# One maximum for both parts of a shared score bank, masks for it by TensorE, and rows of the next batch listed a step ahead of their transposes

## The chip, the cores and the metric

The kernel runs on one core of a Trainium2 chip. The time is the device time of one execution in microseconds (us); less is better. The core's engines work from queues of their own: TensorE (PE in the profile; its weight loads are PEld), VectorE (DVE), ScalarE (ACT), GpSimd (POOL), and SyncE (SP), which issues DMAs here. TensorE writes into PSUM, which has eight banks of 128 partitions by 512 float32 values; an engine waits where it needs data or a buffer that another still holds.

## The reference

A transformer block with adaptive layer norms: attention, then a mixture of experts, over 4 batches of 1024 tokens of width 256.

```python
h = _layernorm(x) * (1 + ca) + sa
x = x + ga * attention(h)          # 16 heads of width 16, causal
h = _layernorm(x) * (1 + cb) + sb
x = x + gb * experts(h)            # 8 experts, the two best of each token

# attention
scores = jnp.einsum('bhqd,bhkd->bhqk', Q, K) / np.sqrt(D_HEAD)
causal = jnp.triu(jnp.full((t, t), -jnp.inf), k=1)
attn = jax.nn.softmax(scores + causal, axis=-1)
O = jnp.einsum('bhqk,bhkd->bhqd', attn, V)
```

The softmax subtracts each query's largest score. The kernel needs that maximum before it computes the scores that it exponentiates, and this is the work that the change touches.

## The kernel before

The attention runs over 16 units: unit u is batch u // 4 and, within it, four heads (`qd` = u % 4). Scores are computed twice. The first time (`m_parts`, L822) queries lie on the partitions, and VectorE takes each query's maximum over the keys (`maxima`, L837). `max_rows` (L857) turns the maxima into rows with a transpose on TensorE and writes them by DMA into a spare row of the query tile. The second time (`s_parts`, L889) keys lie on the partitions, the spare row subtracts the maximum inside the matmul, ScalarE takes the exponential (`weigh`, `exponential`), and `av_step` (L924) multiplies by the values.

A unit has nine steps. In step i, `both` (L1087) does the exponentiated scores of unit u and the maxima of unit u + 1, in two halves of two heads each. A half-step on TensorE is: two score banks and two maxima banks filled in turn, the masks on the scores (L913), then the value product of the step before (first half), or a piece of other work (second half). Each head has a contraction of 32 rows, so four matmuls run side by side in the array. A matmul in float32 is two records in the profile.

All these banks, and those of smaller work (`misc`), come from one pool of seven PSUM buffers, `ps_sc`. A bank is free again when ACT has taken its exponential or DVE its maximum.

`m_steps` (L801) says which query tile (128 queries) and key half (512 keys) each step's maxima bank holds, as (query tile, key half, first column). Causality leaves some tiles narrow, and in steps 1, 2 and 8 two of them share a bank: 384 + 128, 256 + 256, and 384 + 128 columns. The last 128 columns of a tile on the diagonal need the triangular mask. In `both` VectorE adds the mask in the same custom operation that takes the maximum (L851), one per part and head, each followed by a read of its accumulator; tiles off the diagonal take a plain reduction (L849, tile `mf`), and the second key half's maximum includes the first's through `mf`. Before unit 1's third step, `m_alone` (L870) does maxima with TensorE adding the masks (L878). There, and on the scores, a mask is a bf16 matmul of an identity and the mask (`unit`, `qmask`).

The other work is kept in queues, and a few pieces are taken after each step. `todo` has the next batch's layer norm and projections: `ln_pieces` (L719) gives the statistics and four pieces, one per half of the tokens and half of the width, that transpose normalized rows; then come query and key projections (`qk_pieces`) and value projections (`v_pieces`). The rows `xn` of one half (`normalized`, L62, four operations of VectorE) are made in the first piece of that half, in a tile with one buffer (`xnp`). `spread` (L786) sends projected queries and keys by DMA to the tiles of a unit, two units ahead. The number of pieces after a step is what is left divided by the steps left, rounded up; in the last batch it is two. `gates`, `choices` and `sends` are further queues, with the gates of the attention and the routing.

The order in the text is not wholly the order on the engines: the compiler's scheduler may move an instruction ahead of others of its engine where its data allow it. Statistics and row operations can so come earlier than they are written.

After the attention (from about 760 us) comes the expert stage, which the change does not touch.

Of the kernel before, what the change touches and what calls it, by code (L numbers as in the profile page):

```python
# [9 lines left out]
F32 = mybir.dt.float32  # L10
# [51 lines left out]
def normalized(nc, pool, x_b, mv, rs, half, tag):  # L62

    xn = pool.tile([P, 4, D], F32, tag=f"xn{tag}", name=f"xn{tag}")
    for i in range(4):
        t = 4 * half + i
        nc.vector.tensor_scalar(
            xn[:, i, :], x_b[:, t, :], mv[:, t, 0:1], rs[:, t : t + 1], ALU.subtract, ALU.mult
        )
    return xn  # L70
# [10 lines left out]
def adaln_block_kernel(  # L81
# [495 lines left out]
    with ExitStack() as actx:  # L577
# [130 lines left out]
        def blank_rows():  # L708
# [7 lines left out]
            for rows in (blank, slots[JUNK : JUNK + BLK, :]):  # L716
                nc.sync.dma_start(out=rows.rearrange("(p j) d -> p j d", p=P), in_=fill)

        def ln_pieces(b):  # L719
            def begin():  # L720
                st["ln", b], pieces = layer_norm_pieces(nc, small, xs[b], eps, "a")
                for f in pieces:
                    f()
                st["hT", b] = htp.tile([P, NDC, T], F32, tag="hT", name="hT")

            def piece(half, dc):
                def run():
                    if dc == 0:
                        st["xn", b] = normalized(nc, xnp, xs[b], *st["ln", b], half, "a")
                        if b == 0 and half == 0:  # L730
                            modulated(st.pop("ps_m"))
                    transposed(
                        nc, misc(), st["xn", b], dc, ident,
                        st["hT", b][:, dc, half * 512 : (half + 1) * 512],
                        scale1[:, dc, b : b + 1], modT[:, dc, b : b + 1],
                    )

                return run

            out = [piece(h, dc) for h in range(NH) for dc in range(NDC)]  # L740
            return [lambda f=out[0]: (begin(), f())] + out[1:]
# [44 lines left out]
        def spread(u):  # L786
# [16 lines left out]
            [(4, 0, 0)], [(6, 0, 0)], [(7, 0, 0)], [(7, 1, 0)], [(6, 1, 0), (4, 1, 384)],  # L803
        ]

        s_steps = [
            [(0, 0, 0)], [(0, 1, 0), (0, 3, 384)], [(0, 2, 0), (1, 6, 256)],
            *([(1, kt, 0)] for kt in range(5)), [(1, 5, 0), (1, 7, 384)],
# [3 lines left out]
        def in_turn(*heads):  # L812

            for k in range(max(map(len, heads))):
                for parts in heads:
                    for f in parts[k : k + 1]:
                        f()
# [4 lines left out]
        def m_parts(u, i, j, open_end=False):  # L822

            ps, r = bank("ps_max"), HW * j

            def fill(k):
                qt, kb, at = m_steps[i][k]
                n = m_size(qt, kb)
                nc.tensor.matmul(  # L829
                    ps[:, at : at + n], qTs[u % 3][r : r + HW, qt * P : (qt + 1) * P],  # L830
                    kTs[u % 3][r : r + HW, kb * 512 : kb * 512 + n],
                    start=(k == 0), stop=(k == len(m_steps[i]) - 1 and not open_end),
                )

            return ps, [lambda k=k: fill(k) for k in range(len(m_steps[i]))]

        def maxima(u, i, j, ps, masked=()):  # L837

            for part in sorted(m_steps[i], key=lambda part: (part in masked, part[2]), reverse=True):
                qt, kb, at = part
                half, n = qt // 4, m_size(qt, kb)
                kind = ("mx", u, half) if kb == half else ("mf", u)
                if kind not in st:
                    st[kind] = mxp.tile([P, 4, 4], F32, tag=kind[0], name=kind[0])
                top = st[kind][:, j, qt % 4 : qt % 4 + 1]
                if kb < half or part in masked:
                    nc.vector.tensor_reduce(top, ps[:, at : at + n], AX.X, ALU.max)  # L849
                else:  # L850
                    nc.vector.tensor_tensor_reduce(  # L851
                        out=unused[:, 0:n], in0=ps[:, at : at + n], in1=cmask[:, 512 - n : 512], scale=1.0,
                        scalar=st["mf", u][:, j, qt % 4 : qt % 4 + 1] if kb else MASKED,
                        op0=ALU.add, op1=ALU.max, accum_out=top,
                    )

        def max_rows(u, half):  # L857

# [207 lines left out]

        todo = deque()
        soon = deque()

        gates, choices, sends = deque(), deque(), deque()  # L1070
        pending = None
# [15 lines left out]
        def both(u, i, u_max, i_max):  # L1087

            pts = []
            for h in range(2):  # L1090
                scores, tops, parts = [], [], []
                for j in (2 * h, 2 * h + 1):
                    for of, banks in ((s_parts(u, i, j), scores), (m_parts(u_max, i_max, (j + 2) % 4), tops)):
                        banks.append(of[0])
                        parts.append(of[1])
                in_turn(*parts)
                for k in range(2):
                    maxima(u_max, i_max, (2 * h + k + 2) % 4, tops[k])
                pts.extend(weigh(i, scores, h == 0))

                if h == 0 and pending is not None:
                    finish(pending)
            return u, i, pts


# [32 lines left out]
        for u in range(NU):  # L1138
            b, qd = divmod(u, NQD)
            if u + 2 < NU:  # L1140
                spread(u + 2)()
            if u > 0 and qd == 0 and b + 1 < B:
                st["rest"] = ln_pieces(b + 1) + qk_pieces(b + 1, 0), v_pieces(b + 1) + qk_pieces(b + 1, 1)
            if b + 1 < B:
                one, two = st["rest"]
                if u > 0:
                    todo.extend((one[:10], one[10:], two[:10], two[10:])[qd])
            if qd == 1 and 0 < b < B - 1:
                todo.extend(wo_pieces(b - 1))
            if qd == 0:  # L1150
                biases, weights = gate_pieces(b)
                if u > 0:
                    gates.extend(biases)
            if qd == 2 and b < B - 1:
                gates.extend(weights)
            if u == NU - 2:
                for k in range(B):
                    nc.sync.dma_start(out=gb[:, k, :], in_=mods[k, 1, :].partition_broadcast(P))
            if qd == 2 and 0 < b < B - 1:
                choices, sends = map(deque, route_pieces(b - 1, misc))  # L1160
            for i in range(BEGUN if u == 0 else 0, len(s_steps)):
# [12 lines left out]
                if (b, qd, i) == (B - 1, 1, 4):  # L1174
                    gates.extend(weights)

                pending = both(u, i, u + 1, i) if u + 1 < NU else four_heads(u, i)
                if u + 1 < NU and i == 4:
                    todo.appendleft(max_rows(u + 1, 0))

                if gates:
                    gates.popleft()()
                while soon and soon[0][0] <= step:
                    soon.popleft()[1]()

                for _ in range(2 if b == B - 1 else -(-len(todo) // (len(s_steps) - i))):
                    if todo:
                        todo.popleft()()
                early = b == B - 1 and (qd, i) < (1, 2)
                sending = early or not choices  # L1190
                for _ in range(1 if early else 2 - i % 2 if b > 1 else 1 + (i % 3 == 2)):
                    if choices and not (early and len(choices) < 19):
                        choices.popleft()()
                for _ in range(2 if u + 1 == NU or u == NU - 4 and i % 2 else 1):
                    if sends and sending:
                        sends.popleft()()
                step += 1
            while b + 1 < B and len(todo) > 1:
                todo.popleft()()
            if u + 1 < NU:  # L1200
                todo.appendleft(max_rows(u + 1, 1))
# [161 lines left out]
```

## Time and profile before

| | us |
|---|---|
| median of 3 runs | 1061.35 (1058.91 to 1062.14) |
| the profiled execution | 1067.35 |
| its span, first to last instruction | 1065.6 |
| TensorE busy in the span | 1009.5 (95%) |
| VectorE busy | 750.8 (70%) |
| ScalarE busy | 509.7 (48%) |
| plain maxima, L849, of 512 columns, 256 of them | 164.0 |
| maxima with mask, L851, of four widths, 488 of them | 254.8 (140.5 and 114.3 in two groups) |
| masks on the scores, L913, 1328 of them | 57.5 |

The profile is one execution. Its page has the span in 40 equal slices (26.6 us each), a digit for each engine's busy share in tenths. Groups are instructions of one line, engine and shape: count, total busy time, mean of one in nanoseconds, idle time before them and what ended it. A timeline is in order of time: start, length, engine, line, what is written and read, count of merged instructions, and idle time before. Matmuls overlap in the array, so a record's length is more than its share of the engine's time; the distance from one start to the next is what a matmul costs when TensorE is full.

### The profile page before, as it was taken

How to read it: one execution, taken by the hardware profiler on the slowest of the kernel's cores; microseconds unless marked ns; L12 is line 12 of the kernel's file. 1: busy time of each engine (PE TensorE's matmuls, PEld its weight loads, DVE VectorE, ACT ScalarE, POOL GpSimd, SP SyncE). 2: the span in 40 equal slices, each digit the busy share in tenths (PEclk: the TensorE clock that was granted, in tenths of full speed). 3: DMA queues.
4: the chain of work that ended last, by engine and by line, in shares of the span. 5: the costliest groups of instructions: out<-in, count | busy, mean ns of one | idle time of the engine just before them, and what ended most of it. 6: DMA issues, size and time to landing. Idle time of an engine off the chain costs nothing. (4 is left out here: it accounts for less than half of the span.)

```text
span 1065.6 us, 22453 instructions
## 1 busy us (share of the span) xinstructions
PE 1009.5 (95%) x8154; PEld 597.5 (56%) x8154; DVE 750.8 (70%) x2349; ACT 509.7 (48%) x963; POOL 239.5 (22%) x231
## 2 busy tenths in 40 slices
PE   5899999999999999999999999998689999999994
PEld 4554534544544544454463444533368888888893
DVE  4787867766787877788868788782466686566761
ACT  4125654655555555655545546446313264444540
POOL 4000010000000001222001330015131764444344
PEclk9899999999999999999999999999889999999997
DMA  8310120110111202123010331002489956443432
GB/s 272 82 31 8 38 47 14 35 39 14 38 46 49 56 24 48 45 65 86 19 42 28 78 83 36 22 28 72 135 260 289 314 105 158 72 66 65 66 62 25
DMA packets 68686, 81.58 MB, mean 77 GB/s; under 512 B 19480, under 2 KB 50072, under 8 KB 68448
## 3 DMA queue, kind: packets, MB, share of 16 engines
q1 hardware_dynamic: 55008, 63.26, 21.7%
q0 software_dynamic: 13296, 16.89, 8.9%
q8 instruction: 64, 1.05, 0.4%
q14 instruction: 46, 0.38, 0.1%
q10 hardware_dynamic: 272, 0.00, 0.0%
HBM read 45.11 MB, written 24.93 MB: 66 GB/s over the span
## 5 line engine op out<-in xcount | busy, mean ns | idle before, releaser
L921 ACT ACTIVATE pt<-ps_s 128x512 f32<-128x512 f32 x576 | 313.0, 596 | 295.0 <-PE ps_s L913 183.2
L829 PE MATMUL ps_max<-kT,qT 32*128 32x512 f32 (+3 forms) x1536 | 376.6, 531 | 4.6 <-DVE mf L849 2.9
L896 PE MATMUL ps_s<-qT,kT 32*128 32x512 f32 (+3 forms) x1536 | 343.9, 527 | 4.2 <-DMA qT<-rows 2.4
L896 PEld LDWEIGHTS ps_s<-qT,kT 32*128 32x128 f32 x1536 | 134.5, 186 | 143.3 <-issue 44.9
L849 DVE TENSOR_REDUCE mf<-ps_max 128x1 f32<-128x512 f32 x256 | 164.0, 682 | 60.4 <-PE ps_max L829 55.2
L851 DVE CUSTOM_DVE_ANT_0 unused<-ps_max,cmask,mf 128x256 f32<-128x256 f32 (+3 forms) x256 | 140.5, 549 | 46.9 <-PE ps_max L829 27.1
L829 PEld LDWEIGHTS ps_max<-kT,qT 32*128 32x128 f32 x1536 | 153.4, 188 | 34.3 <-DVE mx L851 11.0
L940 PE MATMUL av<-pt,vaug 128*32 128x512 f32 (+3 forms) x1536 | 160.3, 505 | 0.8 <-ACT ot L948 0.8
L972 POOL TENSOR_TENSOR oc<-oc,rec 64x512 f32<-64x512 f32 x32 | 40.6, 1270 | 506.9 <-DMA rec<-inv 453.8
L567 POOL DMA_INDIRECT out_dram<-y,xb x67 | 107.8, 1609 | 131.1 <-DVE gs L529 55.7
L851 DVE CUSTOM_DVE_ANT_0 unused<-ps_max,cmask 128x128 f32<-128x128 f32 (+2 forms) x232 | 114.3, 493 | 29.5 <-PE ps_max L829 15.1
L550 PE MATMUL ps_h<-xt,wa 128*128 128x256 f32 (+1 forms) x608 | 125.2, 358 | 1.3 <-DVE xt L538 1.3
L561 PE MATMUL ps_y<-wb,hs 128*128 128x256 f32 x536 | 122.7, 379 | 0.0
L550 PEld LDWEIGHTS ps_h<-xt,wa 128*128 128x128 f32 x608 | 103.6, 193 | 12.3 <-DVE xt L538 1.6
L561 PEld LDWEIGHTS ps_y<-wb,hs 128*128 128x128 f32 x536 | 100.6, 190 | 13.2 <-ACT hs L554 0.2
L529 DVE SCALAR_TENSOR_TENSOR gs<-x,share,gs 128x256 f32<-128x256 f32 x201 | 85.2, 477 | 1.0
L554 ACT ACTIVATE hs<-ps_h 128x512 f32<-128x512 f32 x67 | 39.8, 597 | 86.4 <-PE ps_h L550 76.9
L940 PEld LDWEIGHTS av<-pt,vaug 128*32 128x32 f32 x1536 | 38.1, 112 | 76.4 <-issue 67.4
L343 POOL DMA_INDIRECT slots<-hr,sloti x64 | 63.7, 995 | 76.5 <-ACT sloti L342 55.5
L566 DVE TENSOR_TENSOR y<-ps_y,gs 128x256 f32<-128x256 f32 x67 | 25.9, 419 | 72.2 <-PE ps_y L561 69.6
L913 PEld LDWEIGHTS <-qmask 128*32 128x32 bf16 (+1 forms) x1328 | 30.2, 97 | 66.6 <-issue 59.1
L913 PE MATMUL ps_s<-unit,qmask 128*32 128x128 bf16 (+1 forms) x1328 | 57.5, 227 | 0.1
(220 smaller groups left out, 924.2 us busy)
## 6 DMA issues: line engine op xcount, KB each, us to landing
w_s<-in_w_dram SPq DMA_DIRECT2D x16, 512.0 KB
xb<-slots SPq DMA_DIRECT2D x29, 259.0 KB
qT<-qc SPq DMA_DIRECT2D x64, 64.0 KB
kT<-kc SPq DMA_DIRECT2D x64, 64.0 KB
oc<-ot SPq DMA_DIRECT2D x128, 32.0 KB
rec<-inv SPq DMA_DIRECT2D x32, 128.0 KB
out_dram<-x SPq DMA_DIRECT2D x8, 512.0 KB
wa<-in_w_dram SPq DMA_DIRECT2D x8, 512.0 KB
```

Source lines behind the costliest of these rows:

```text
L343: sent = nc.gpsimd.indirect_dma_start(out=slots, out_offset=bass.IndirectOffsetOnAxis(ap=at, axis=0), in_=hr[:, t, :], in_offset=None,).ins
L529: nc.vector.scalar_tensor_tensor(gs[:, j, :], gb[:, b, :], share[:, j, b : b + 1], gs[:, j, :], ALU.mult, ALU.add)
L550: nc.tensor.matmul(ps[:, k, :], w[:, dc, fc * P : (fc + 1) * P], xt[:, dc, :], start=(dc == 0), stop=(dc == NDC - 1),)
L561: nc.tensor.matmul(ps[:, j, :], hs[:, fc, j * P : (j + 1) * P], w[:, fc, :], start=(fc == 0), stop=(fc == NFC - 1),)
L567: added = nc.gpsimd.indirect_dma_start(out=out_rows, out_offset=bass.IndirectOffsetOnAxis(ap=xb[:, j, D : D + 1].bitcast(I32), axis=0), in ...
L829: nc.tensor.matmul(ps[:, at : at + n], qTs[u % 3][r : r + HW, qt * P : (qt + 1) * P], kTs[u % 3][r : r + HW, kb * 512 : kb * 512 + n], sta ...
L849: nc.vector.tensor_reduce(top, ps[:, at : at + n], AX.X, ALU.max)
L851: nc.vector.tensor_tensor_reduce(out=unused[:, 0:n], in0=ps[:, at : at + n], in1=cmask[:, 512 - n : 512], scale=1.0, scalar=st["mf", u][:, ...
L896: nc.tensor.matmul(ps[:, at : at + n], kTs[u % 3][r : r + HW, kt * P : (kt + 1) * P], qTs[u % 3][r : r + HW, (qb + 1) * 512 - n : (qb + 1) ...
L913: nc.tensor.matmul(ps[k : k + w, at : at + P], qmask[:, k : k + w], unit, start=False, stop=at == masked[-1],)
L921: nc.scalar.activation(pt[:, 0:n], ps[:, 0:n], AF.Exp)
L940: nc.tensor.matmul(av[HW * j : HW * (j + 1), 512 - n : 512], vaug[b % 2][:, kt, 4 * qd + j, :], pts[j][:, at : at + n], start=(kt == 0), s ...
```

## The change

It has three parts.

**Maxima of two parts at once.** For units above 4 (`joint`), the steps whose bank holds two parts let TensorE add the masks to the maxima banks, and VectorE takes one plain reduction over the whole bank into two or four maxima (`joint_maxima`), as a bank of 256 + 256 or as four pieces of 128. Partial maxima of the 384-column tile go to a tile `mp`; `join` reduces and combines them after steps 2 and 8. Both halves' maxima lie in one tile `mx2`. Steps 0 and 3 change places for these units, so that one half is whole after step 2.

**Statistics in units 1 and 2.** The layer norm statistics of batches 2 and 3 are listed one piece per step from unit 1 on.

**Rows a step ahead.** For batches 2 and 3 the first half's rows are listed at the end of the unit before, and the second half's right behind the last transposes of the first half, a step ahead of their own transposes. In the first four steps of the units at which a batch's projections begin (4 and 8), one piece is taken per step, two in the first.

```diff
+        m_joint = [m_steps[3], *m_steps[1:3], m_steps[0], *m_steps[4:]]
+        def joint(u):
+            return u > NQD
+        def m_list(u):
+            return m_joint if joint(u) else m_steps
...
+        def joint_maxima(u, i, j, ps):
+            tops_of(u)
+            if m_size(*m_joint[i][0][:2]) == 256:
+                out, n = st["mx2", u][:, :, j, 1], 256
+            else:
+                out, n = st["mp", u, m_joint[i][0][0] // 4][:, j, :], P
+            nc.vector.tensor_reduce(out, ps.rearrange("p (a n) -> p a n", n=n), AX.X, ALU.max)
+
+        def join(u, half):
+            mx, mp = st["mx", u, half], st.pop(("mp", u, half))
+            nc.vector.tensor_reduce(mx[:, :, 2], mp[:, :, 0:3], AX.X, ALU.max)
+            if half == 0:
+                nc.vector.tensor_copy(mx[:, :, 0], mp[:, :, 3])
+            else:
+                mf = st["mf", u]
+                nc.vector.tensor_tensor(mx[:, :, 0], mp[:, :, 3], mf[:, :, 0], ALU.max)
+                nc.vector.tensor_tensor(mx[:, :, 1:3], mx[:, :, 1:3], mf[:, :, 1:3], ALU.max)
...
+            two = joint(u_max) and len(m_joint[i_max]) > 1
...
                 in_turn(*parts)
+                if two:
+                    w = P if h else HW
+                    for ps in tops:
+                        for part in m_joint[i_max]:
+                            at = part[2] + m_size(*part[:2]) - P
+                            for k in range(0, P, w):
+                                nc.tensor.matmul(
+                                    ps[k : k + w, at : at + P], unit[:, k : k + w], qmask,
+                                    start=False, stop=part == m_joint[i_max][-1],
+                                )
                 for k in range(2):
-                    maxima(u_max, i_max, (2 * h + k + 2) % 4, tops[k])
+                    (joint_maxima if two else maxima)(u_max, i_max, (2 * h + k + 2) % 4, tops[k])
...
+            if joint(u_max) and i_max in (2, 8):
+                join(u_max, i_max // 8)
...
+        stats = deque()
+        for b in range(2, B):
+            st["ln", b], pieces = layer_norm_pieces(nc, small, xs[b], eps, "a")
+            stats.extend(pieces)
...
-                    if dc == 0:
-                        st["xn", b] = normalized(nc, xnp, xs[b], *st["ln", b], half, "a")
+                    if dc == 0 and b < 2:
+                        rows_of(b, half)
...
+                    if b > 1 and (half, dc) == (0, NDC - 1):
+                        rows_of(b, 1)
...
-                for _ in range(2 if b == B - 1 else -(-len(todo) // (len(s_steps) - i))):
+                turning = u > 0 and qd == 0 and b + 1 < B and i < 4
+                for _ in range(2 if b == B - 1 else 1 + (i == 0) if turning else -(-len(todo) // (len(s_steps) - i))):
                     if todo:
                         todo.popleft()()
+                if u > 0 and stats:
+                    stats.popleft()()
+                if qd == NQD - 1 and b + 2 < B and i == 7:
+                    rows_of(b + 2, 0)
```

More of the change, by code (lines that the diff above doesn't have):

```diff
@@ L717, in blank_rows, with rows_of @@
                 nc.sync.dma_start(out=rows.rearrange("(p j) d -> p j d", p=P), in_=fill)
+        def rows_of(b, half):
+            st["xn", b] = normalized(nc, xnp, xs[b], *st["ln", b], half, "a")
         def ln_pieces(b):
             def begin():
-                st["ln", b], pieces = layer_norm_pieces(nc, small, xs[b], eps, "a")
-                for f in pieces:
-                    f()
+                if b < 2:
+                    st["ln", b], pieces = layer_norm_pieces(nc, small, xs[b], eps, "a")
+                    for f in pieces:
+                        f()
                 st["hT", b] = htp.tile([P, NDC, T], F32, tag="hT", name="hT")
@@ L826, in fill @@
             def fill(k):
-                qt, kb, at = m_steps[i][k]
+                qt, kb, at = m_list(u)[i][k]
                 n = m_size(qt, kb)
@@ L831, in fill @@
                     kTs[u % 3][r : r + HW, kb * 512 : kb * 512 + n],
-                    start=(k == 0), stop=(k == len(m_steps[i]) - 1 and not open_end),
+                    start=(k == 0), stop=(k == len(m_list(u)[i]) - 1 and not open_end),
                 )
-            return ps, [lambda k=k: fill(k) for k in range(len(m_steps[i]))]
+            return ps, [lambda k=k: fill(k) for k in range(len(m_list(u)[i]))]
         def maxima(u, i, j, ps, masked=()):
-            for part in sorted(m_steps[i], key=lambda part: (part in masked, part[2]), reverse=True):
+            for part in sorted(m_list(u)[i], key=lambda part: (part in masked, part[2]), reverse=True):
                 qt, kb, at = part
@@ L844, in maxima @@
                 kind = ("mx", u, half) if kb == half else ("mf", u)
+                if joint(u) and kind[0] == "mx":
+                    tops_of(u)
                 if kind not in st:
@@ L855, in maxima, with tops_of @@
                     )
+        def tops_of(u):
+            if ("mx", u, 0) not in st:
+                both_halves = mxp.tile([P, 2, 4, 4], F32, tag="mx2", name="mx2")
+                for half in range(2):
+                    st["mx", u, half] = both_halves[:, half]
+                    st["mp", u, half] = mxp.tile([P, 4, 4], F32, tag=f"mp{half}", name="mp")
+                st["mx2", u] = both_halves
+        def joint_maxima(u, i, j, ps):
+            tops_of(u)
+            if m_size(*m_joint[i][0][:2]) == 256:
[12 more added lines that the diff above has]
+                nc.vector.tensor_tensor(mx[:, :, 1:3], mx[:, :, 1:3], mf[:, :, 1:3], ALU.max)
         def max_rows(u, half):
@@ L1068, in adaln_block_kernel @@
         soon = deque()
+        stats = deque()
+        for b in range(2, B):
+            st["ln", b], pieces = layer_norm_pieces(nc, small, xs[b], eps, "a")
+            stats.extend(pieces)
         gates, choices, sends = deque(), deque(), deque()
@@ L1092, in both @@
                 for j in (2 * h, 2 * h + 1):
-                    for of, banks in ((s_parts(u, i, j), scores), (m_parts(u_max, i_max, (j + 2) % 4), tops)):
+                    for of, banks in ((s_parts(u, i, j), scores), (m_parts(u_max, i_max, (j + 2) % 4, two), tops)):
                         banks.append(of[0])
```

## The prediction

> **What bounds the kernel now.** I read the page's busy table and slices first, then the groups with shapes kept apart, the waits, and TensorE's (PE's) timeline through the units that the change touches.
>
> ```profile
> PE   5899999999999999999999999998689999999994
> ...
> DVE  4787867766787877788868788782466686566761
> ```
>
> TensorE (busy 95% of the span) is full from the second slice on, VectorE (DVE, 70%) at 7 to 8 tenths until slice 28 (750 us). The chain that ended last is only the tail's scatter, so it says nothing of the attention. "Full" hides something: matmuls overlap, so a short stall leaves no idle time. I therefore measured, in PE's timeline, each half-step of `both` from its first score matmul to whatever follows the group. Undisturbed it is 1.07 us (300.05 to 301.13). The change acts from 237 us (maxima of unit 5, taken during unit 4) to 728 us. There the 198 half-steps' groups take 55 us more than 1.07 each: 26.5 us before 586 us, 28.7 us in the last three units after it. PE is the bound, and DVE makes it late in places:
>
> ```profile
> PEld ps_s L896 <- DVE mx L851: 27.1, 54, 1.5
> ...
> PEld ps_s L896 <- ACT pt L921: 25.0, 60, 1.6
> ```
>
> (us in total, times, longest.) These waits are for banks of the seven-buffer score pool that the masked maxima or the exponentials still hold.
>
> **Masks on TensorE: the cost.** In units 5 to 15, steps 1, 2 and 8 hold two maxima parts per bank. Each such step gains 16 mask matmuls 32 columns wide (first half) and 4 full ones (second half): 11 x 3 x 20 = 660. Their nearest row is the same mask on the scores:
>
> ```profile
> 316.23 0.41 PE L913 MATMUL ps_s<-unit,qmask 128*32 128x128 bf16 x16
> 316.46 1.03 PE L940 MATMUL av<-pt,vaug 128*32 128x512 f32 x8
> ...
> 318.84 0.40 PE L913 MATMUL ps_s<-unit,qmask 128*128 128x128 bf16 x4
> 319.07 1.08 PE L1003 MATMUL ps_mi<-wg,oc 128*128 128x256 f32 x4
> ```
>
> Start to next start: 0.23 us for sixteen narrow ones, 0.23 us for four full ones. All three steps already have score masks of the same width in the same half, so the new ones join an existing run of that form. So 0.46 us a step, 33 steps: **+15.2 us**. Here the Trainium skill speaks against the change ("TensorE: Matmul & The Clock Gate", section "Wait — 56ns, not 53.3ns?"): however small a matmul, starts are never under about 25 ns apart. Sixteen would then take 0.40 us and the sum be (0.40 + 0.23) x 33 = 20.8 us. The row shows sixteen in 0.23 us, four at a time in different columns of the array, so I take the row and keep 20.8 as the far end. The near end is 0: masks issued while PE would wait for DVE anyway cost nothing.
>
> **One maximum per bank: what it takes off DVE.**
>
> ```profile
> L849 DVE TENSOR_REDUCE mf<-ps_max 128x1 f32<-128x512 f32 x256 | 164.0, 682 | 60.4 <-PE ps_max L829 55.2 <-PE ps_s L896 2.1 <-issue 1.6
> ```
>
> ```profile
> 690.59 0.48 DVE L851 CUSTOM_DVE_ANT_0 unused<-ps_max,cmask,mf 128x256 f32<-128x256 f32 x1
> 691.11 0.42 DVE L851 CUSTOM_DVE_ANT_0 unused<-ps_max,cmask 128x256 f32<-128x256 f32 x1
> 691.68 0.48 DVE L851 CUSTOM_DVE_ANT_0 unused<-ps_max,cmask,mf 128x256 f32<-128x256 f32 x1
> ```
>
> Two masked maxima with their accumulator reads take 1.09 us a head at step 2 (690.59 to 691.68), by the same timeline 1.05 at step 1 and 1.16 at step 8 (232.15 to 233.31): 3.3 us, times four heads 13.2 us a unit. Three plain reductions of 512 at 0.68 each are 8.2 us. The five joining operations have no row; the small ones nearest (128x8 sums 180 ns, 128x64 summed into 8, 216 ns) give 1.0 us a unit, between 0.7 and 1.2. DVE loses 13.2 - 8.2 - 1.0 = 4.0 us a unit, 44 us in all; a bank is held 0.68 us after its fill, not 1.05 to 1.16. Joins wait for nothing but DVE itself and have DVE's free quarter for cover; without it they cost 11 us.
>
> What this is worth at PE is a choice. Going through the 55 us half-step by half-step, outside the two turns treated below, I count as DVE's the stalls in and just after steps 1, 2 and 8 whose weight load waited for a masked maximum: about 9 us in the first eight units, 16 in the last three. An example, seen in the weight loads of step 3 of the last pair of units:
>
> ```profile
> 698.17 0.29 PEld L896 LDWEIGHTS ps_s<-qT,kT 32*128 32x128 f32 x2 [1.53 <-DVE mx L851]
> 698.89 0.29 PEld L829 LDWEIGHTS ps_max<-kT,qT 32*128 32x128 f32 x2 [0.43 <-ACT pt L921]
> ```
>
> Once the masked maximum lets go, the exponential (ACT) is next late, by 0.43 here. So not all comes back: I take two thirds of 9, **-6 us**, and three quarters of 16, **-12 us**, since in those last units little projection work remains for PE between the groups, while DVE still has routing to do (39.3 of 49 us busy from 678 to 727). Ends: none of it, and all 25.
>
> **The turns (rows and spread pieces).** At the start of units 4 and 8 the next batch's second half of normalized rows is late. The transposes, in order on PE, wait for it and are scattered between the groups (at 243.16, 244.21 and 245.41):
>
> ```profile
> 242.01 0.83 PE L940 MATMUL av<-pt,vaug 128*32 128x384 f32 x2
> 243.16 0.30 PE L76 MATMUL ps_mi<-ident,xna 128*128 128x128 f32 x1 [0.31 <-DVE xna L67]
> ...
> 246.99 1.92 PE L940 MATMUL av<-pt,vaug 128*32 128x384 f32 x14
> ...
> 248.84 0.73 PE L896 MATMUL ps_s<-qT,kT 32*128 32x256 f32 x1
> ```
>
> From 242.01 to 248.84 PE does work that undisturbed takes 0.97 (values) + 0.54 (transposes) + 1.08 (group) + 0.23 (masks) = 2.82 us: 4.0 lost. The second turn (419.39 to 426.10) loses 3.9. In the changed program's compiled order those transposes stand together again, one step later, and the four row operations stand a step ahead of them. The rows wait for the earlier transposes, which PE issues before DVE gets there; behind them on DVE are that step's maxima, late by 4 x 0.33 us as they were. **-8 us**; ends 0 (the wait returns one step on) and -9. The projections pushed back (L773, with the DMAs of L794 that need them) have the rest of two units before `spread` wants them: nothing.
>
> **The statistics: nothing.** The compiled order of both programs has all four batches' statistics at the very start, and the trace agrees (view of line 44):
>
> ```profile
> L44 DVE BATCH_NORM_STATS2 sta<-x x32: 381/396/428, 5.0 to 39.8; 128x6 f32<-128x256 f32 x32
> ```
>
> Listing them in units 1 and 2 moves no instruction. Swapping steps 0 and 3 costs the same operations; the first half's maxima are now whole at step 2, two steps (some 9 us) ahead of their transpose at step 4. Score exponentials of the three steps come 0.23 us later behind the new masks, which is in the 15.2. SP and POOL get the same DMAs.
>
> **The clock.** The granted clock falls to half for 3.4 us at a time at 246, 423, 649, 669 and 700 us, each time just after the stalls above. The first three lie in stalls already counted. The skill's page (section "HAM oscillation") makes idle gaps above about 3.4 us the cause; no stall here passes 1.6 us, so by that rule nothing comes back. The trace shows the dips where PE was thinned out by shorter ones, so I give half of the last two (3.4 us at half speed is 1.7 each): **-2 us**; ends 0 and -3.4.
>
> **Sum.** 15.2 - 6 - 12 - 8 - 2 = -12.8 us. The profiled execution took 1067.35 us, its span 1065.6; so a span near 1053. The median shown is 1061.35, 6 us under that execution. The difference is carried over: **1048.5 us**.
>
> **Rivals.** (1) *TensorE pays and nothing comes back* (slower). The stall only changes its owner: a bank freed early by DVE is still waited for, because its neighbour in the rotation holds scores until ACT's exponential ends. For it: 25.0 us of waits are ACT's, and PE looks 9 tenths full throughout. Against: the longest stalls name DVE. It decides where relief and clock together stay under 15.2 - 8 = 7.2 us; with none, 1061.35 + 7.2 = 1068.5. (2) *Full relief*: all 25 us of DVE's stalls, both dips, 9 at the turns: 15.2 - 25 - 3.4 - 9 = -22, and up to 5 more where DVE's lag also delayed fillers: 1034 to 1039. For it: DVE falls from 80% to some 72% there. Against: PE's own work does not shrink. (3) *The turns don't mend*, the wait moving to the next transposes: 8 us less gain, 1056.5. For it: one row buffer serves both halves. Against: the compiled order.
>
> **How the numbers follow.** Forecast 0.53, rival 1 0.18, rival 2 0.17, rival 3 0.12. 0.3% is 3.2 us, about what a measurement tells from no change. The forecast's own spread gives faster 0.48, same 0.04, slower 0.01; rival 2 all faster; rival 3 0.07, 0.03, 0.02; rival 1 same 0.03, slower 0.15. Together 0.72, 0.10, 0.18. Range 1034 to 1067: down to full relief, up to little relief with the masks at their row's price.
>
> **What would show it.** Right: 660 new mask rows adding about 0.23 us per half-step; the groups' 55 us of excess falling below 35; turns without scattered transposes; DVE some 40 us less busy; fewer half-clock stretches between 640 and 730. Wrong: units 6, 7, 10 and 11 longer by far more than 0.5 us each, waits for ACT taking DVE's place after 586 us, or masks at 0.4 us per sixteen.

## The result, and the profile after

| | before | after |
|---|---|---|
| median of the runs taken together, us | 1061.45 (10 runs) | 1069.04 (10 runs) |
| lowest to highest | 1058.03 to 1073.84 | 1064.34 to 1073.48 |
| ratio, with 95% interval | | 1.0058 [1.0031, 1.0085] |

The changed kernel is slower, by 3 to 9 us. It lies above the predicted range, at the number worked out for the first rival (TensorE pays and nothing comes back: 1068.5); whether by that rival's mechanism is asked below. The profiled execution of the changed kernel took 1064.34 us, the fastest of its ten, and that of before 1067.35, slow for its kernel. The spans of the two profiles (1062.6 and 1065.6) would therefore tell the opposite of the truth; they are not compared here.

The page of the changed kernel, busy times and slices:

```profile
PE 1006.0 (95%) x8814; PEld 604.9 (57%) x8814; DVE 724.7 (68%) x2008; ACT 508.6 (48%) x963; POOL 238.5 (22%) x231
...
PE   5899999999999999999999999998689999999993
...
DVE  4787777767686667667767688682466686566761
```

TensorE has 660 more instructions (8154 before). DVE falls by 26 us (750.8 before), not by some 40: the prediction took a masked pair from start to next start, 1.09 us a head, and its records cover 0.92. DVE's slices between 240 and 586 us stand mostly at 6 and 7 where they were mostly at 7 and 8. TensorE's digits don't move, but for the last. The groups of the page (count, then busy time, mean in ns, then idle time before):

```profile
L867 DVE TENSOR_REDUCE mf<-ps_max 128x1 f32<-128x512 f32 x256 | 164.1, 683 | 61.1 <-PE ps_max L845 55.2
...
L890 DVE TENSOR_REDUCE mp<-ps_max 128x4 f32<-128x512 f32 x88 | 56.6, 684 | 38.3 <-PE ps_max L1154 34.8
```

L890 is the new joint maximum: four results of 128 columns cost what one result of 512 does, 684 against 683 ns. In this group, the banks of four pieces, DVE now waits 34.8 us for the new masks (L1154): it stands ready before TensorE has filled and masked the bank. The masks themselves, in TensorE's timeline of unit 14's step 1:

```profile
637.10 0.41 PE L1154 MATMUL ps_max<-qmask,unit 128*32 128x128 bf16 x16
637.33 0.40 PE L959 MATMUL ps_s<-unit,qmask 128*32 128x128 bf16 x16
637.55 1.03 PE L986 MATMUL av<-pt,vaug 128*32 128x512 f32 x8
...
639.60 0.40 PE L1154 MATMUL ps_max<-qmask,unit 128*128 128x128 bf16 x4
639.83 0.39 PE L959 MATMUL ps_s<-unit,qmask 128*128 128x128 bf16 x4
640.05 1.08 PE L1049 MATMUL ps_mi<-wg,oc 128*128 128x256 f32 x4
```

From start to next start the new masks take 0.23 us for sixteen narrow ones and 0.23 for four full ones, as the row of before said. And the waits between 237 and 586 us, of before (us in total, times, longest):

```profile
PEld ps_s L896 <- ACT pt L921: 14.6, 36, 0.8
PEld ps_s L896 <- DVE mx L851: 11.7, 30, 0.8
```

The same view of after:

```profile
DVE mp L890 <- PE ps_max L1154: 27.1, 26, 1.5
...
PEld ps_s L942 <- ACT pt L967: 12.8, 31, 0.8
...
PEld ps_s L942 <- DVE mp L890: 5.0, 6, 0.8
...
PEld ps_s L942 <- DVE mx L869: 2.1, 7, 0.3
```

The score weight loads waited 11.7 us for a masked maximum; now they wait 2.1 us for those that are left and 5.0 for joint ones, 4.6 us less. Yet most of these units got longer. To see where the time is, a measure is needed that depends less on the run.

**The measure.** A unit's time is taken from TensorE's timeline, from the first maxima matmul of one unit to that of the next; the unit is the one whose maxima are taken, so the turns at the start of units 4 and 8 lie in columns 5 and 9. Steps count from 0. The profile records stretches in which the granted clock is half; half of such time is subtracted. Where no half-clock stretch falls in a unit or step, the number mostly repeats between runs and chips to 0.01 or 0.02 us (step 1 of unit 6: 5.72 or 5.73 us in before and in each kernel that leaves this step alone). The sum over units 5 to 15 is good to about 2 us, because the correction for the clock is rough.

One place where it fails can be put right. In before, steps 6 and 7 of unit 15 take 3.56 and 5.80 us, with a wait in the second:

```profile
715.72 0.18 PEld L896 LDWEIGHTS ps_s<-qT,kT 32*128 32x128 f32 x1 [1.14 <-DVE mf L849]
```

In after a half-clock stretch covers most of step 6; the steps take 5.04 and 4.33 us, and this wait is gone. The two steps together are 9.36 and 9.37: the stretch cost nothing, as it took up a time in which TensorE waits otherwise. The table subtracts half of it all the same, so its sums for after and e3_masks, where the same happened, are 1.9 us too low.

| unit | 5 | 6 | 7 | 8 | 9 | 10 | 11 | 12 | 13 | 14 | 15 | sum |
|---|---|---|---|---|---|---|---|---|---|---|---|---|
| before | 44.50 | 41.59 | 46.40 | 43.62 | 42.80 | 41.87 | 45.32 | 45.68 | 43.91 | 43.48 | 44.38 | 483.6 |
| after | 43.17 | 42.52 | 47.67 | 44.70 | 42.49 | 42.51 | 46.66 | 46.24 | 42.25 | 44.22 | 42.30 | 484.7 |
| e1_turns | 42.41 | 41.58 | 46.38 | 43.62 | 41.98 | 41.58 | 45.32 | 45.96 | 43.58 | 43.73 | 44.37 | 480.5 |
| e2_joint | 45.16 | 42.52 | 47.74 | 44.87 | 44.59 | 42.80 | 46.67 | 45.75 | 42.37 | 43.91 | 44.12 | 490.5 |
| e3_masks | 44.62 | 42.27 | 47.82 | 44.78 | 43.44 | 42.27 | 46.25 | 46.51 | 43.02 | 44.35 | 44.51 | 489.8 |
| f2_pinned | 42.69 | 42.52 | 47.65 | 44.72 | 42.01 | 42.52 | 46.67 | 45.42 | 42.26 | 42.57 | 43.61 | 482.6 |

The pattern is plain. Units 6, 7, 8, 10 and 11 are longer by 0.6 to 1.3 us each (three masked steps cost 3 x 0.45 = 1.36). Units 5 and 9, with the turns, are shorter by 1.3 and 0.3. Of the last three, two are shorter by 1.7 and 2.1, of which 1.9 in unit 15 is the clock effect just described and not the change. So put right, after is 3.0 us longer than before.

### The profile page after: what moved, and what is told of

Same layout as the page of the kernel before. It is cut to its first block, busy times and chain, and to the rows that moved or that the text cites. A ratio compares the mean times of both kernels' runs of the same rounds, so it can differ in the third digit from the quotient of the medians.

```text
span 1062.6 us, 23313 instructions
## 1 busy us (share of the span) xinstructions
PE 1006.0 (95%) x8814; PEld 604.9 (57%) x8814; DVE 724.7 (68%) x2008; ACT 508.6 (48%) x963; POOL 238.5 (22%) x231
## 5 line engine op out<-in xcount | busy, mean ns | idle before, releaser
L845 PE MATMUL ps_max<-kT,qT 32*128 32x512 f32 (+3 forms) x1536 | 369.2, 530 | 8.0 <-DVE mf L867 4.1
L942 PE MATMUL ps_s<-qT,kT 32*128 32x512 f32 (+3 forms) x1536 | 339.7, 528 | 2.9 <-DMA qT<-rows 2.9
L942 PEld LDWEIGHTS ps_s<-qT,kT 32*128 32x128 f32 x1536 | 131.9, 185 | 138.0 <-issue 50.1
L867 DVE TENSOR_REDUCE mf<-ps_max 128x1 f32<-128x512 f32 x256 | 164.1, 683 | 61.1 <-PE ps_max L845 55.2
L845 PEld LDWEIGHTS ps_max<-kT,qT 32*128 32x128 f32 x1536 | 150.3, 186 | 34.4 <-DVE mf L867 6.2
L986 PE MATMUL av<-pt,vaug 128*32 128x512 f32 (+3 forms) x1536 | 157.1, 502 | 0.8 <-ACT ot L994 0.8
L869 DVE CUSTOM_DVE_ANT_0 unused<-ps_max,cmask,mf 128x512 f32<-128x512 f32 (+2 forms) x124 | 76.7, 619 | 25.5 <-PE ps_max L845 16.2
L890 DVE TENSOR_REDUCE mp<-ps_max 128x4 f32<-128x512 f32 x88 | 56.6, 684 | 38.3 <-PE ps_max L1154 34.8
L869 DVE CUSTOM_DVE_ANT_0 unused<-ps_max,cmask 128x512 f32<-128x512 f32 (+2 forms) x100 | 58.3, 583 | 21.9 <-PE ps_max L845 14.7
L959 PEld LDWEIGHTS <-qmask 128*32 128x32 bf16 (+1 forms) x1328 | 32.5, 98 | 55.4 <-issue 53.3
```

Source lines behind the costliest of these rows:

```text
L845: nc.tensor.matmul(ps[:, at : at + n], qTs[u % 3][r : r + HW, qt * P : (qt + 1) * P], kTs[u % 3][r : r + HW, kb * 512 : kb * 512 + n], sta ...
L869: nc.vector.tensor_tensor_reduce(out=unused[:, 0:n], in0=ps[:, at : at + n], in1=cmask[:, 512 - n : 512], scale=1.0, scalar=st["mf", u][:, ...
L890: nc.vector.tensor_reduce(out, ps.rearrange("p (a n) -> p a n", n=n), AX.X, ALU.max)
L942: nc.tensor.matmul(ps[:, at : at + n], kTs[u % 3][r : r + HW, kt * P : (kt + 1) * P], qTs[u % 3][r : r + HW, (qb + 1) * 512 - n : (qb + 1) ...
L986: nc.tensor.matmul(av[HW * j : HW * (j + 1), 512 - n : 512], vaug[b % 2][:, kt, 4 * qd + j, :], pts[j][:, at : at + n], start=(kt == 0), s ...
```

## Experiments: which part costs, which part pays

Two accounts stood against each other. In one, the masks are paid in full and VectorE's relief comes back only in part, the turns being the only sure gain. In the other, the relief does come back, and something else, the turns or the new order, spoils it. The first four kernels take the change apart. They ran on one chip, beside 38 runs of before with a median of 1062.99 us.

**Turns alone.** Without joint maxima, with rows, statistics and the slower taking of pieces kept:

```diff
         def joint(u):
-            return u > NQD
+            return False
```

> The rows a step ahead, the spread pieces and the listed statistics alone; the masked maxima stay on VectorE as before. Forecast's theory: the turns are worth 8 us, so ratio about 0.992 (1053). Rival 'the turns don't mend': 1.000. From the two traces (steps 1 to 5 of units 5 and 9 in the profile after, 2 to 3.4 us shorter each once the masks are allowed for): 4 to 7 us, ratio 0.9935 to 0.996.

Measured: 1058.71 us, ratio 0.9963 [0.9941, 0.9984]: faster, by 2 to 6 us. By units the gain is 3.1 us: 2.1 in unit 5, 0.8 in unit 9. Step by step in unit 9, before and then here: step 1 6.09 and 4.71, step 2 5.84 and 5.54, step 3 4.11 and 3.66, step 4 4.64 and 5.08, step 5 4.39 and 5.25. The transposes stand together again, in TensorE's timeline of this kernel at unit 5:

```profile
239.05 0.61 PE L76 MATMUL ps_mi<-ident,xna 128*128 128x128 f32 x4
...
243.29 0.48 PE L845 MATMUL ps_max<-kT,qT 32*128 32x256 f32 x1 [0.45 <-DVE mx L869]
...
244.59 0.61 PE L76 MATMUL ps_mi<-ident,xna 128*128 128x128 f32 x4
```

The prediction's stall is gone, but the projection pieces that were taken earlier before are still work: 0.86 us of it turns up in step 5 of both units. The middle line is a stall that is left, 0.45 us for a masked maximum.

**Joint maxima alone.** The order of pieces, rows and transposes as before (`turning = False`, `rows_of` called where the rows were made; the statistics too stand where they stood, in lines not shown):

```diff
-                    if dc == 0 and b < 2:
+                    if dc == 0:
                         rows_of(b, half)
...
-                    if b > 1 and (half, dc) == (0, NDC - 1):
-                        rows_of(b, 1)
...
-                turning = u > 0 and qd == 0 and b + 1 < B and i < 4
+                turning = False
```

> The joint maxima with masks by TensorE alone, turns and statistics as before. Forecast's theory (15 paid, 18 to 20 back): ratio 0.995 to 0.997. Rival 'TensorE pays and nothing comes back': 1.010 to 1.014, since the change as a whole is 1.0058 and the turns are worth 4 to 8 us.

Measured: 1073.70 us, ratio 1.0087 [1.0058, 1.0115], slower by 6 to 12 us; by units 6.9 longer. The masks have 33 x 0.455 = 15.0 to pay, so 8.1 us come back: 10.9 - 8.3 = 2.6 in units 5 to 12, and 4.1 + 1.4 = 5.5 in units 13 to 15. The next run shows how much of this is owed to VectorE's relief.

**Masks alone.** The kernel before, with the new masks on TensorE; VectorE's operations stay as many and as long, and add a mask of zeros:

```diff
+    zmask = ctile([P, 512], "zmask")
+    nc.gpsimd.memset(zmask, 0.0)
...
-                        out=unused[:, 0:n], in0=ps[:, at : at + n], in1=cmask[:, 512 - n : 512], scale=1.0,
+                        out=unused[:, 0:n], in0=ps[:, at : at + n], in1=(zmask if added else cmask)[:, 512 - n : 512], scale=1.0,
...
+            two = u_max > NQD and len(m_steps[i_max]) > 1
...
+                if two:
+                    w = P if h else HW
+                    for ps in tops:
+                        for part in m_steps[i_max]:
...
-                    maxima(u_max, i_max, (2 * h + k + 2) % 4, tops[k])
+                    maxima(u_max, i_max, (2 * h + k + 2) % 4, tops[k], added=two)
```

> Masks by TensorE added to the two-part maxima banks, and VectorE's work kept as it was: the same custom operations with a mask of zeros, in the old step order. The price of the masks with no relief for VectorE: 15.2 us by the scores' mask row, ratio 1.0143; nearer 1.005 if most masks fall where TensorE would wait for VectorE anyway. The relief is this run minus the joint maxima alone: 18 us by the forecast, 0 to 4 us by rival 1.

Measured: 1068.80 us, ratio 1.0057 [1.0034, 1.0081]; by units 8.1 longer (6.2 in the table, 1.9 for unit 15), not 15.0. This is the most telling run. With VectorE as loaded as ever, 6.9 of the masks' 15.0 us fall into time in which TensorE waits anyway. With VectorE relieved (joint alone) the kernel is 6.9 us longer than before. So the relief, this run minus that one, is worth 1.2 us and not 18: 3.4 are won in the last three units and 2.1 lost in the others, most of these in units 5 and 9. The timed runs agree. Brought to a mean granted clock of 0.972 by a line through each kernel's own runs, both take 1072.1 us, and before takes 1063.6 (rough, as the lines rest on 6 and 7 runs).

The prediction had named both effects, masks that lie in waits (its near end of 0) and waits that relief removes. The two runs fit one stock of waiting time that can be spent once: masks that fill a wait leave nothing for relief to remove, and relief that removes it leaves the masks bare. That this is all is not shown; the next section finds relief that was lost in another way.

**Joint maxima in the last batch only.**

```diff
-            return u > NQD
+            return u > 3 * NQD
```

> The change with the joint maxima only in the last three units (above 12), turns as changed. Forecast's theory: 4.1 paid and 12 to 14 back there, 8 at the turns: ratio 0.983. Rival 1: no more than the turns alone, plus up to 4 us: 0.995 to 0.999.

Measured: 1062.13 us, ratio 0.9959 [0.9936, 0.9982]. Units 5 to 11 are those of turns alone to 0.01 us. Units 13 to 15 sum to 131.05 us, turns alone 131.68: masks paid, 0.6 us gained. The gain in the last batch exists, and is small, as the first account has it.

## Experiments: what fills VectorE's freed time

The prediction expected 12 of its 18 us of relief in the last three units, in and just after the masked steps. But of these step 2 got longer in units 12, 14 and 15: 4.64, 4.32 and 5.33 us before, 6.86, 6.43 and 6.23 after. VectorE's timeline of after at unit 14 shows why there; the bank was full and masked at about 642.6 us:

```profile
642.43 0.42 DVE L44 BATCH_NORM_STATS2 stb<-x 128x6 f32<-128x256 f32 x1
...
643.10 0.17 DVE L49 TENSOR_SCALAR veb<-mvb 128x8 f32<-128x8 f32 x1
643.43 0.20 DVE L51 RECIPROCAL rsb<-rsb 128x8 f32<-128x8 f32 x1 [0.16 <-ACT rsb L50]
643.67 0.17 DVE L54 TENSOR_TENSOR nwb<-rsb 128x8 f32<-128x8 f32 x1
...
644.74 0.48 DVE L240 SCALAR_TENSOR_TENSOR hr<-x,mvb,md 128x256 f32<-128x256 f32 x1 [0.30 <-issue]
645.15 1.28 DVE L890 TENSOR_REDUCE mx<-ps_max 128x2 f32<-128x512 f32 x2
```

The weight loads of after, right behind the first of these two maxima:

```profile
645.89 0.18 PEld L845 LDWEIGHTS ps_max<-kT,qT 32*128 32x128 f32 x1 [2.02 <-DVE mx L890]
```

Nine operations of the second layer norm, none over 0.48 us, stand in one row ahead of the maximum that TensorE waits for. In before, the same chain is threaded between the masked maxima, one small operation after each:

```profile
643.02 0.17 DVE L49 TENSOR_SCALAR veb<-mvb 128x8 f32<-128x8 f32 x1
643.11 0.48 DVE L851 CUSTOM_DVE_ANT_0 unused<-ps_max,cmask,mf 128x256 f32<-128x256 f32 x1
...
643.51 0.20 DVE L51 RECIPROCAL rsb<-rsb 128x8 f32<-128x8 f32 x1
643.63 0.42 DVE L851 CUSTOM_DVE_ANT_0 unused<-ps_max,cmask 128x256 f32<-128x256 f32 x1
...
643.98 0.16 DVE L54 TENSOR_TENSOR nwb<-rsb 128x8 f32<-128x8 f32 x1
```

In units 12 and 15 it is other work: the join and the routing. In unit 12 of after the bank was full and masked at about 557.8 us, and nine operations stand in a row ahead of its maximum, three of them shown:

```profile
556.35 0.68 DVE L275 TENSOR_TENSOR gt<-lg 128x512 f32<-128x512 f32 x1
...
557.02 0.16 DVE L897 COPY mx<-mp 128x4 f32<-128x4 f32 x1
...
559.75 0.22 DVE L295 TENSOR_REDUCE top<-pr 128x8 f32<-128x64 f32 x1
559.88 1.28 DVE L890 TENSOR_REDUCE mx<-ps_max 128x2 f32<-128x512 f32 x2
```

Nothing in the source says so; the compiler's scheduler ordered it. Freed time alone does not explain it: in masks alone, where VectorE does as much as before, most of the chain stands ahead of unit 14's maxima too, and that step takes 5.80 us.

The next runs test this, on a second chip (before: 1069.06 us in 53 runs, where unit 13 took 1 to 3 us more than elsewhere in each kernel, and unit 10 about 1 in the first two), and then together on a third (before: 1066.15 us in 33 runs).

**Order of steps.** Steps 0 and 3 are not swapped (`m_joint = m_steps`), the rest as in the change.

> The change, with steps 0 and 3 left in their old places for all units. Theory now held (the masks are paid in full in the middle units, and the masked maximum of step 0 makes step 1 wait longer): step 1 of units 6, 7, 10 and 11 falls from 0.54-0.71 us over before to 0.45, 1 to 2 us in all: ratio 1.003 to 1.005. If the swap costs nothing: 1.0058 as the change.

Measured: 1074.41 us, ratio 1.0046 [1.0027, 1.0066]. Step 1 of units 6, 7 and 11 falls to 0.45 over before, as expected. But units 5 and 6 get shorter by only 0.25 us each, unit 9 longer by 0.23, and the others that can be compared hardly change: the swap explains little of the loss.

**Pinned order.** The change, with the chain and the join held in the order in which the source has them among VectorE's other ordered work:

```diff
-        nc.vector.tensor_scalar(ve, mv[:, :, 1], EPS, None, ALU.add)
+        pin(nc.vector.tensor_scalar(ve, mv[:, :, 1], EPS, None, ALU.add))
...
-        nc.vector.reciprocal(rs, rs)
+        pin(nc.vector.reciprocal(rs, rs))
...
-            nc.vector.tensor_reduce(mx[:, :, 2], mp[:, :, 0:3], AX.X, ALU.max)
+            in_order(nc.vector.tensor_reduce(mx[:, :, 2], mp[:, :, 0:3], AX.X, ALU.max))
...
-                nc.vector.tensor_copy(mx[:, :, 0], mp[:, :, 3])
+                in_order(nc.vector.tensor_copy(mx[:, :, 0], mp[:, :, 3]))
```

(`pin` is `in_order` for the second layer norm and does nothing for the first.) Chain and join are held together, so what each is worth is not separated.

> The change, with the joining operations and the second layer norm's inverse held behind the joint maxima in VectorE's order; nothing else moves. Theory now held (other work placed ahead of the joint maxima of step 2 makes TensorE wait there): the stalls of 1.8, 2.3 and 1.6 us in step 2 of units 12, 14 and 15 go or shrink below 0.8: 3 to 5 us, ratio 1.001 to 1.003. If those waits only return a step later: 1.005 to 1.006.

Measured: 1069.85 us, ratio 1.0000 [0.9981, 1.0018]: level with before. As the change itself did not run on that chip, both were run side by side on the third:

> The change itself once more, on one chip with the three runs that follow, since two chips differed by 6 us in the kernel before. Unit times (half of the half-clock time taken off) add up in units 5 to 15 to 1 to 2 us over the kernel before; ratio 1.003 to 1.0085.

> The change with the joining operations and the second layer norm's inverse held behind the joint maxima, again. If other work ahead of the joint maxima costs what the profile shows: 3 to 5 us under the change on this chip, most of it in units 12, 14 and 15. If the earlier gap was the chip's or the clock's: within 1.5 us of the change.

Measured: the change 1071.45 us, ratio 1.0044 [1.0023, 1.0066]; pinned 1064.88, ratio 0.9989 [0.9968, 1.0011]. The pin is worth 6.6 us of time, 4.5 of it at a mean clock of 0.972 (1069.4 and 1064.9, by a line through each kernel's own runs), and 4.0 to 5.2 by units, the change taken from its first profile or from this one and unit 15 put right. VectorE's timeline of the pinned kernel at the same place:

```profile
644.03 1.29 DVE L890 TENSOR_REDUCE mx<-ps_max 128x2 f32<-128x512 f32 x2 [0.22 <-PE ps_max L1154]
646.51 1.29 DVE L890 TENSOR_REDUCE mx<-ps_max 128x2 f32<-128x512 f32 x2 [1.19 <-PE ps_max L1154]
...
647.85 0.17 DVE L49 TENSOR_SCALAR veb<-mvb 128x8 f32<-128x8 f32 x1
647.93 0.20 DVE L51 RECIPROCAL rsb<-rsb 128x8 f32<-128x8 f32 x1
```

Both pairs of maxima now stand ahead of the chain, and DVE waits for TensorE. In units 12 and 15 the join, and most of the routing with it, now comes behind them. Step 2 of units 12, 14 and 15 takes 5.05, 4.13 and 4.65 us. Not all of that is won: the chain comes later, and step 4 of units 12 and 15 is 0.9 and 1.1 us longer than in the change. Units 5 and 9 gain 0.5 us each in their step 2 as well, where the join was in the way.

**Last batch only, pinned, and without the swap:**

```diff
-        m_joint = [m_steps[3], *m_steps[1:3], m_steps[0], *m_steps[4:]]
+        m_joint = m_steps
...
-            return u > NQD
+            return u > 3 * NQD
```

> Joint maxima only above unit 12, steps in their old places, held order as in the run before, turns as changed: the version meant to be fastest. Theory: the turns' 3.9 us and 3 to 6 us in the last three units: ratio 0.991 to 0.9945. If the last units gain nothing: 0.996 as the turns alone.

> Joint maxima above unit 12 only, held order, turns. By its unit times 2.4 us under the pieces' pacing alone; by the timed runs before this, 3 us over it, at a lower clock. If the unit times decide: ratio 0.990 to 0.994; if half-clock stretches are drawn by this program oftener: above the pacing alone again and at a mean clock lower by 0.004.

Measured: 1059.33 us, ratio 0.9919 [0.9892, 0.9945] on the second chip; 1056.37 us, ratio 0.9897 [0.9857, 0.9936] on the third. It beats before by about 1%, and on the third chip the change by 1.4%. Its step 2 of unit 14 takes 4.13 us, as in the pinned change.

**Only the taking of pieces.** The kernel before and one line of the change:

```diff
+                turning = u > 0 and qd == 0 and b + 1 < B and i < 4
-                for _ in range(2 if b == B - 1 else -(-len(todo) // (len(s_steps) - i))):
+                for _ in range(2 if b == B - 1 else 1 + (i == 0) if turning else -(-len(todo) // (len(s_steps) - i))):
```

> The kernel before with the number of pieces in the first four steps of units 4 and 8 alone; rows and statistics are listed where they were. Its compiled order on TensorE and VectorE is that of the run with rows and statistics listed ahead, line for line. So the same time as that run: ratio 0.994 to 0.9985, unit times equal to it within 0.05 us where no half-clock stretch falls. Anything else would mean that the listing of rows and statistics matters by another way than order.

> The pieces' pacing at the turns alone, again. Unit times add up to 1.5 to 3 us under the kernel before: ratio 0.994 to 0.998. If it is 0.988 again, pacing is worth more than its unit times say, by the clock.

Measured: 1055.91 us, ratio 0.9883 [0.9844, 0.9923], and 1057.54 us, ratio 0.9917 [0.9889, 0.9945]. Its compiled order on TensorE and VectorE is that of turns alone, instruction for instruction; and with rows and statistics listed early, but without this line, the compiled order is that of before (a program that was not run). So of the second and third part of the change only this line acts. Turns alone gained 0.4% with that same order and these two 1.2 and 0.8%, more than expected. Much of that is the clock: at a mean clock of 0.972, by a line through each kernel's own runs, the three are 3.2, 5.4 and 4.3 us under before on their chips. By units the gain was 3.1. The best kernel is not told apart from this one-line edit: the two intervals on the third chip overlap.

What the relief is worth with no masks on TensorE at all was not measured.

## Why the prediction was wrong, step by step

- **Masks, +15.2: right as a cost.** 0.23 + 0.23 us a step, and undisturbed steps are longer by 0.45. The floor of 25 ns between starts that the prediction cites from the Trainium skill would have made it 20.8; four masks side by side in the array's columns don't obey it. What the near end of 0 stood for, masks inside waits, is real for 6.9 us (masks alone), and is time that the next point takes as well.
- **Relief, -6 and -12: the step that failed.** The prediction charged the masks in full and beside that counted "two thirds of 9" and "three quarters of 16" us of waits as won. Joint alone returned 2.6 and 5.5, 8.1 of 18, and masks alone returned 6.9 with no relief at all. Two things were in the way. First, many named waits held no time of TensorE's: step 2 of units 6 and 10 took 4.60 us before, which is the sum of its parts (2 x 1.07 + 2 x 0.23 + 0.97 + 1.08 = 4.65). Nothing could come back there, and the step is 0.45 longer after. A weight load that waits while the values' product still runs cost TensorE nothing there. Second, the scheduler put the layer norm, the join and the routing ahead of joint maxima that TensorE waited for. The pinned run shows it: against turns alone it returned 5.5 of the 6 (1.36 x 8 - 5.4), and 7.3 of the 12. How the 5 us still missing divide between waits that were never lost time and the rest is open.

  ACT did not take DVE's place. The score weight loads' waits for it before 586 us went from 14.6 to 12.8 us; weight loads' waits for it after 586 us went from 3.8 to 4.5. So the number of rival 1 was nearly met, but not by its mechanism: it had 8 us from the turns and none from relief, where the runs show 2.9 and 8.1.

  The waits of after from 586 to 727 us show the owners that are left:

```profile
PEld ps_max L845 <- DVE mx L890: 4.0, 5, 2.0
...
PEld ps_max L845 <- ACT pt L967: 3.4, 5, 0.7
...
PE ps_max L845 <- DVE mx L890: 2.5, 2, 1.6
```

  DVE is still the largest, now with the joint maximum behind the chain (2.0 us at the longest); no wait for ACT is over 0.7.
- **The turns, -8: right in kind, too large.** Scattered transposes are gone, and the gain is 2.9 us. Of the 4.0 and 3.9 us counted as lost, 1.7 each was a half-clock stretch of 3.4 us inside the very window (step 2 of units 5 and 9). The pieces pushed back, costed at nothing, cost 0.86 in each turn's step 5. 8 - 3.4 - 1.7 = 2.9.
- **Statistics, 0: right.** They lie at 5.1 to 40.1 us in after, at 5.0 to 39.8 in before.
- **The clock, -2: not seen.** Half-clock stretches were taken as a property of the stalls. After has 20.5 us of them in units 5 to 15, before 17.1, and one program, in two profiles on two chips, none and 34.1 (below). Five in one profile said nothing of the next. (The longest stall was a weight load's of 1.8 us, not 1.6; it changes nothing here.)
- **The base.** The difference of 6 us between the profiled execution and the median was carried over whole, while 3.4 us of the turns' 7.9 was half-clock time of that very execution, which the median runs need not have there.

With the measured terms, 15.0 - 8.1 - 2.9 = +4.0 us, where the prediction had -12.8: the relief makes 9.9 us of that gap, the turns 5.1, the clock 2.0. By the table of units, put right, it is 3.0. The medians are 7.6 apart, with 3.3 to 9.0 by the interval. On the third chip both kernels ran at the same mean clock, 0.970; brought to 0.972 by a line through each kernel's own runs, they are 4.9 us apart (1064.5 and 1069.4). So the terms explain the difference at equal clock. What made the medians of the first ten runs lie further apart is not known, as the clocks of the ten runs of before are not on record. Of the signs named, the groups' excess fell from 55.2 to 46.7 us and not below 35; units 7 and 11 grew by 1.3 us; masks were not at 0.4. The prediction gave the case that happened 0.18.

## What to carry to other kernels

Before relief of an engine that is not the bound is counted, compare each step with the sum of its parts on the engine that is: where a step is already at that sum, a named wait is covered and nothing returns, while work added to the bound engine is paid there in full. Where waits are real, added work may hide in them or relief may remove them; test the added work alone before both are counted. And when a change takes work off an engine, look in the compiled order at what stands ahead of its operations that release a buffer: rows of small operations there cost 1.6 to 2.3 us at a time here, and holding the order took most of it away.

## What the runs showed of the hardware

The clock of before and of the kernel that only changes the taking of pieces (its first run), from their pages:

```profile
PEclk9899999999999999999999999999889999999997
```

```profile
PEclk9899999999999999999999999999889999999998
```

The digits hide the difference: in units 5 to 15 the first profile has 17.1 us at half clock, the second none, and the second profile of that same program has 34.1. Stretches are 3.4 us or multiples of it, at other places in each profile. Their share goes with much of the scatter: over 38 runs of before on the first chip, time falls by about 0.9 us for each 0.001 of mean granted clock, and the nine runs of that second program on the third chip have mean clocks from 0.963 to 0.979. Most single steps, by contrast, repeat to 0.02 us between runs, kernels and chips (units 10 and 13 on the second chip do not), which makes them the better measure for a change of this size.

A stretch at half clock need not cost time. Step 7 of unit 15 takes 4.33 or 4.34 us in the seven profiles in which step 6 lies 3.7 us or more at half clock, and 5.80 in the seven in which it has none there, whatever the kernel. In before the 5.80 hold a wait of 1.14 us for VectorE; in after, with the slow step ahead of it, that wait is gone.
